# Haar coefficients left unscaled, thresholds scaled on the chip, products copied by ScalarE

## The chip, the core and the metric

The kernel runs on one core of a Trainium2 chip. The metric is the device time of one execution in microseconds (us). A core has a matrix engine (TensorE, PE in the profile), three engines for elementwise work (VectorE or DVE, ScalarE or ACT, GpSimd or POOL), and SyncE (SP), which here issues all transfers. Sixteen DMA engines carry them. TensorE writes to PSUM, and another engine has to copy the result from there to SBUF, the on-chip memory.

## The reference

The input is x with 4 images, 64 channels and 256 x 256 points in float32. Four layers follow each other. Layers 0, 2 and 3 are long convolutions with a filter that is a product of a row part and a column part; the filters come from a small network with sines:

```python
k = jnp.einsum('ijk,imk->ijmk', hx, hy)[0]           # per channel: a column times a row
y = irfft2(rfft2(x) * rfft2(k) / fft_size)[..., :L, :L]
out = y + x * bias[:, None, None]
```

Layer 1 works on Haar wavelet coefficients. The 2D transform is orthonormal (a factor of 1/sqrt(2) at each of its 8 steps along rows and along columns); channels are mixed with two weight matrices, and the result is shrunk by soft thresholds that differ from point to point but not from channel to channel:

```python
f1 = haar2d(x)
for i in range(2):
    f4 = jnp.einsum('bchw,oc->bohw', f1 * v[i], conv_w[i])
    acc = acc + jnp.sign(f4) * jax.nn.relu(jnp.abs(f4) - tau[i])
y = haar2d(acc, inverse=True) + x
```

## The kernel before

The images form two groups of two. Phase A does layer 0 and the forward Haar transform; phase B does the mixing and the shrinking; phase C does the inverse transform and layers 2 and 3. Between the phases the coefficients go through DRAM (`coef` from A to B, `mixed` and `unshrunk` from B to C), because A and C work by channel and B by position.

**Phase A** has 64 rounds, 32 for each group; a round has 2 channels of 2 images. A round multiplies by Toeplitz matrices on TensorE, first along one axis (PSUM tiles `a1ps`, copied by ScalarE to `ay`, L460), then along the other (`a2ps`, joined with the bias term by VectorE into `x`, L480). Then GpSimd does the Haar transform along the free axis (`forward_free`, L360 and L362), with sums and differences only, and a product with a 64 x 64 Haar matrix (`a3ps`, L324) does most of the other axis. Each of its four PSUM tiles a round is evicted into `f` by `product` (L493), and four DMAs (two in group 1) store `f` to `coef` (L497). The free-axis factors that GpSimd leaves out depend only on the column; `wrow_sb` holds them, one for each of 256 columns, and L493 multiplies by it.

The pieces of a round are written out by hand as lists of small functions, and `beside` interleaves one list with another by count. `later` puts an eviction into the next piece. A piece that issues a DMA does so on SyncE, in program order: an issue that has to wait for a buffer or for data keeps back all later ones. In a round SyncE issues four loads of x (L148, 2 KB rows in group 0), four loads of Toeplitz rows `toep` (L161, 32 partitions each) and the stores of `coef`. While phase A works on group 0, the list `rest` runs beside it: the networks of layers 2 and 3 and twelve stores (`spread`, L278) that write each filter to DRAM in repeated copies.

**Phase B** has 64 steps for each group, two units a step (the two weight matrices). For each step it loads `ft` (512 KB, L564) and a tile `v` with the weights v and the thresholds tau (L577). The host has repeated both for the 64 channels; a row of `in_v` holds v and tau of both units in turn. A unit is: product with the mixing weights (L623), times v (VectorE, L642), sign and magnitude (ScalarE, L648 and L657), minus tau and maximum times sign (VectorE, L662 and L667), sum (GpSimd, L682 to L686), store to `mixed` (L691). For group 1 the second unit of most steps is stored raw (L639, L699) and shrunk later, in phase C, with `v_rows`.

**Phase C** reads `mixed` (L774), scales column levels on ScalarE (`scales`, L378), does the inverse transform on GpSimd (`inverse_free`, L401; on VectorE for the first two rounds, L403) and the two convolutions on TensorE.

Phase A of group 0 runs first, then A of group 1 beside B of group 0, then C of group 0 beside B of group 1, and last C of group 1.

Of the kernel before, what the change touches and what calls it, by code (L numbers as in the profile page):

```python
# [97 lines left out]

@with_exitstack
def conv_haar_kernel(  # L100
    ctx: ExitStack, tc: tile.TileContext, x, zT, w1, wbd, cols, wo, decay, wo_first, decay_first, bias, forward, inverse, wrow, pack, v, v_rows, out
):
    nc = tc.nc
    ctx.enter_context(tc.manual_schedule())
# [180 lines left out]
    nc.sync.dma_start(forward_sb, forward)  # L285
    inverse_sb = const.tile([P, ROW], F32, tag="inverse", name="inverse_sb")
    nc.sync.dma_start(inverse_sb, inverse)
    wrow_sb = const.tile([P, N], F32, tag="wrow", name="wrow_sb")
    nc.sync.dma_start(wrow_sb, wrow.partition_broadcast(P))
    bias_sb = const.tile([P, NL * C], F32, tag="bias", name="bias_sb")  # L290
    nc.sync.dma_start(bias_sb, bias.partition_broadcast(P))

    for p in network([0]):
        p()

    rest = []
    rest.append(lambda: wbd_sb.extend(constant(f"wbd{l}", wbd[:, l], [P, 2, P]) for l in (1, 2)))
# [7 lines left out]
    def half(r):  # L305
        return slice(r * ROW, (r + 1) * ROW)

    def toeplitz(ps, data, t, j):

# [61 lines left out]
        m = half // BLOCKS  # L371
        return src.rearrange("p n (k q) -> p (n k) q", k=BLOCKS)[:, :, m : 2 * m]

    def scales(src):

        half = 2
        while half < N:
            nc.scalar.mul(diffs(src, half), diffs(src, half), math.sqrt(half))  # L378
            yield
            half *= 2  # L380

    def inverse_free(src, dst, name, engine, level):
# [27 lines left out]
    def later(op):  # L410

        waiting.append(op)
# [23 lines left out]
    def phase_a():  # L436


        total = GROUPS * ROUNDS
        st = [dict() for _ in range(total)]  # L440

        def filters(t):
            if t < total:
                st[t]["toep"] = first_toep[t] if t < len(first_toep) else load_toeplitz(0, t)

        def load(t):
            if t < total:
                st[t]["x"] = first_x[t] if t < len(first_x) else load_x(t)

        def rows(t, j):  # L450
            s = st[t]
            if j == 0:
                s["y"] = big("t0", f"ay_{t}", 2)
            if j % 2 == 0:
                s["ps"] = banks(f"a1ps{j}_{t}")
            toeplitz(s["ps"], blocks(s["x"]), filters_x(s["toep"]), j)
            if j % 2:
                for r, ps in enumerate(s["ps"]):
                    y = blocks(s["y"])[:, r, j - 1 : j + 1]
                    later(lambda y=y, ps=ps: nc.scalar.copy(y, ps))  # L460

        def columns(t, j):
            s = st[t]
            if j == 0:
                s["x1"] = big("m0", f"x1_{t}", 2)
            if j % 2 == 0:
                s["ps2"] = banks(f"a2ps{j}_{t}")
            toeplitz(s["ps2"], blocks(s["y"]), filters_y(s["toep"]), j)
            if j % 2:
                for e, ps in enumerate(s["ps2"]):  # L470
                    later(lambda e=e, ps=ps: residual(t, e, j, ps))
            if j == BLOCKS - 1:
                s["fw"] = big("m1", f"fw_{t}", 2)
                s["ops"] = forward_free(s["x1"], s["fw"], f"f{t}_")

        def residual(t, e, j, ps):
            s = st[t]
            c = t % ROUNDS * CI + e
            to, old = (blocks(s[name])[:, e, j - 1 : j + 1] for name in ("x1", "x"))
            nc.vector.scalar_tensor_tensor(to, old, bias_sb[:, c : c + 1], ps, ALU.mult, ALU.add)  # L480

        def product(t, bp):
            s = st[t]
            if bp == 0:

                s["f"] = big("out", f"f_{t}", 2)
            two = banks(f"a3ps{bp}_{t}")
            fw = blocks(s["fw"])
            haar(two, lambda r, c: fw[half(r), c, 2 * bp : 2 * bp + 2], forward_sb)
            for b, ps in enumerate(two):  # L490
                f = s["f"][:, 4 * bp + 2 * b : 4 * bp + 2 * b + 2]
                w = wrow_sb.unsqueeze(1).to_broadcast([P, 2, N])
                later(lambda f=f, ps=ps, w=w: nc.vector.tensor_tensor(f, ps, w, ALU.mult))  # L493

        def store(t):
            for to, f in all_rows(coef[t // ROUNDS], t % ROUNDS, st[t]["f"], t >= ROUNDS):
                nc.sync.dma_start(to, f)  # L497
# [36 lines left out]
        t = total - 1  # L534
        end = [lambda: (flush(), run(st[t]["ops"], 16), store(t - 1))]
        end += [lambda bp=bp: (flush(), product(t, bp)) for bp in range(2)]
        end.append(lambda: (flush(), store(t)))
        return pieces, last, end

    def phase_b(grp):  # L540
# [25 lines left out]
        def load_v(s):  # L566
            if s >= STEPS:
                return
            d = st[s]
            d["v"], d["tau"] = [], []  # L570

            def fetch(first, count, tag):
                n = 2 * count * W
# [4 lines left out]
                d["v"] += [t[:, i, 0] for i in range(count)]  # L578
                d["tau"] += [t[:, i, 1] for i in range(count)]
# [176 lines left out]
    def phase_c():  # L756
# [29 lines left out]

        def scale_rows():
            for k in range(2):
                for op in scales(late["rows"][:, k].rearrange("p s (h k) -> p (s h) k", h=2)):
                    pass  # L790

        def shrink(t, k):
# [353 lines left out]
```

## Time and profile before

| | |
|---|---|
| median of 3 runs | 2545.4 us (2540.11 to 2548.39) |
| profiled execution | 2543.18 us, span 2541.3 us |
| mean granted TensorE clock | 0.979 |
| PE, PEld busy | 2311.6 us (91%), 1875.9 us (74%) |
| DVE, ACT, POOL busy | 1840.0 (72%), 1325.9 (52%), 2063.0 us (81%) |
| transfers | 679.08 MB, 267 GB/s on average |
| L493, the multiplication by `wrow_sb` | 256 on VectorE, 161.3 us, 682 ns each |
| `v<-in_v` | 64 of 1024 KB (group 0), 64 of 512 KB (group 1) |

The busy share of an engine is an average over four stages with different limits, so the stages have to be read one by one: a window of the trace gives each engine's busy time in that stretch, the clock that TensorE was granted, the mean busy share of the 16 DMA engines, and what they moved. Idle time of an engine that doesn't set the pace costs nothing. SyncE's issue times show when a transfer was asked for, not when it moved.

### The profile page before, as it was taken

The numbers are of one execution on the slowest core, as the hardware profiler recorded it, in microseconds if no ns is written. First come the engines' busy times: TensorE is split into PE (matmuls) and PEld (weight loads), VectorE is DVE, ScalarE is ACT, GpSimd is POOL, SyncE is SP. The second block draws the span as 40 slices with busy tenths as digits, with TensorE's granted clock in tenths as the row PEclk, the third lists the DMA queues.
The fourth block names the chain that finished last, engine by engine and source line by source line (L and its number), as shares of the span: only waits on it lengthen the run. The fifth ranks groups of instructions, "written<-read, shape, count | busy, mean of one in ns | idle before, by whom it ended". The sixth has DMA issues, their size and how long they took to land.

```text
span 2541.3 us, 118857 instructions
## 1 busy us (share of the span) xinstructions
PE 2311.6 (91%) x53298; PEld 1875.9 (74%) x53298; DVE 1840.0 (72%) x2070; ACT 1325.9 (52%) x2190; POOL 2063.0 (81%) x2428
## 2 busy tenths in 40 slices
PE   7999998788888888877999999999989999999999
PEld 5799996444454444555777777787889999998888
DVE  4655557799999999856777677776667777777763
ACT  1122223566666666244666666666655555556552
POOL 2889997989899999768777767676779999999990
PEclk9999999899999999888999999999999999999999
DMA  6678877799999999556888889889866666666653
GB/s 201 224 269 271 272 275 296 266 327 338 337 320 341 336 318 340 206 184 248 318 320 313 306 302 321 311 312 315 287 215 217 216 215 217 215 212 207 220 167 111
DMA packets 201798, 679.08 MB, mean 267 GB/s; under 512 B 29119, under 2 KB 30464, under 8 KB 188873
## 3 DMA queue, kind: packets, MB, share of 16 engines
q1 hardware_dynamic: 201288, 671.48, 76.3%
q8 instruction: 419, 6.86, 1.1%
q14 instruction: 91, 0.74, 0.1%
HBM read 427.63 MB, written 243.73 MB: 264 GB/s over the span
## 4 chain that ended last, share of the span: by engine, by line
PE 44%; DVE 4%; issue 2%; ACT 2%; DMA 2%; POOL 2%; SPq 1%; DVEq 0%; ACTq 0%; POOLq 0%
PE c2c L312 10%; PE c2r L312 10%; PE c1r L312 9%; PE c1c L312 8%; PE c0ps L324 4%; PE f L623 3%; DVE cy L896 1%; DVE m L667 1%; DMA g<-mixed 1%; DVE x L642 1%; DVE x L662 1%; ACT ch L877 1%; POOL i L401 1%; ACT x L657 0%; SPq L161 0%
## 5 line engine op out<-in xcount | busy, mean ns | idle before, releaser
L401 POOL TENSOR_TENSOR i<-i,g 128x16 f32<-128x16 f32 x744 | 429.9, 598 | 28.2 <-ACT g L378 1.1
L312 PEld LDWEIGHTS a2ps<-toep,ay 64*64 64x64 f32 x8192 | 315.3, 136 | 126.3 <-DVE f L493 70.0
L623 PE MATMUL f<-ft,mix 64*64 64x512 f32 x2048 | 301.7, 623 | 116.8 <-DVE x L642 99.2
L312 PE MATMUL a2ps<-toep,ay 64*64 64x128 f32 (+3 forms) x8192 | 352.8, 303 | 27.4 <-DVE f L493 27.4
L312 PEld LDWEIGHTS a1ps<-toep,x 64*64 64x64 f32 x8192 | 300.1, 134 | 66.3 <-issue 31.8
L312 PE MATMUL a1ps<-toep,x 64*64 64x64 f32 (+3 forms) x8192 | 338.1, 299 | 4.3 <-DMA toep<-filt 2.3
L312 PEld LDWEIGHTS c2c<-toep,ch 64*64 64x64 f32 x8192 | 296.8, 135 | 61.0 <-issue 28.4
L312 PEld LDWEIGHTS c1c<-toep,ch 64*64 64x64 f32 x8192 | 295.4, 133 | 52.0 <-issue 23.7
L685 POOL TENSOR_TENSOR gt<-m,ft 128x512 f32<-128x512 f32 x128 | 163.3, 1276 | 197.8 <-DVE m L667 193.5
L312 PE MATMUL c1r<-toep,z 64*64 64x64 f32 (+3 forms) x8192 | 315.0, 300 | 7.8 <-issue 3.8
L312 PEld LDWEIGHTS c1r<-toep,z 64*64 64x64 f32 x8192 | 291.2, 135 | 41.5 <-issue 19.0
L312 PE MATMUL c2c<-toep,ch 64*64 64x128 f32 (+3 forms) x8192 | 310.0, 299 | 8.6 <-ACT ch L877 6.9
L312 PE MATMUL c2r<-toep,cy 64*64 64x128 f32 (+3 forms) x8192 | 310.1, 298 | 7.9 <-issue 6.6
L312 PEld LDWEIGHTS c2r<-toep,cy 64*64 64x64 f32 x8192 | 288.9, 134 | 37.6 <-issue 20.4
L401 POOL TENSOR_TENSOR ci<-i,g 128x1024 f32<-128x1024 f32 x124 | 312.1, 2539 | 4.5
L648 ACT ACTIVATE m<-x 128x1024 f32<-128x1024 f32 x194 | 206.0, 1062 | 210.0 <-DVE x L642 103.1
L312 PE MATMUL c1c<-toep,ch 64*64 64x128 f32 (+3 forms) x8192 | 307.3, 297 | 4.1 <-ACT ch L877 2.5
L460 ACT COPY ay<-a1ps 128x512 f32<-128x512 f32 x256 | 137.3, 589 | 325.2 <-PE a1ps L312 324.6
L877 ACT COPY ch<-c2r 128x512 f32<-128x512 f32 x256 | 137.2, 589 | 285.2 <-PE c2r L312 284.4
L493 DVE TENSOR_TENSOR f<-a3ps,wrow_sb 128x512 f32<-128x512 f32 x256 | 161.3, 682 | 122.5 <-PE a3ps L324 118.6
L642 DVE TENSOR_TENSOR x<-f,v 128x1024 f32<-128x1024 f32 x192 | 233.4, 1216 | 18.1 <-PE f L623 15.3
L896 DVE SCALAR_TENSOR_TENSOR o<-cy,bias_sb,c2c 128x512 f32<-128x512 f32 x256 | 176.9, 742 | 91.8 <-PE c2c L312 87.1
(84 smaller groups left out, 3950.7 us busy)
## 6 DMA issues: line engine op xcount, KB each, us to landing
toep<-filt SPq DMA_DIRECT2D x768, 112.0 KB
ft<-coef SPq DMA_DIRECT2D x128, 512.0 KB
v<-in_v SPq DMA_DIRECT2D x64, 1024.0 KB
mixed<-gt SPq DMA_DIRECT2D x128, 512.0 KB
g<-mixed SPq DMA_DIRECT2D x256, 256.0 KB
x<-in_x SPq DMA_DIRECT2D x128, 256.0 KB
coef<-f SPq DMA_DIRECT2D x128, 256.0 KB
x<-in_x SPq DMA_DIRECT2D x32, 1024.0 KB
```

Of the source, the lines that this page charges most:

```text
L312: nc.tensor.matmul(ps[r][half(c), j % 2, k * ROW :], data[half(r), c, k, bass.ts(j, ROW)], t(r, c)[:, : N - k * ROW], start=k == 0, stop=k ...
L324: nc.tensor.matmul(ps[r][half(c)].rearrange("p h k -> p (h k)"), matrix[half(r)], pairs(r, c).rearrange("p h k -> p (h k)"), start=True, s ...
L401: engine.tensor_tensor(to, s, d, op)
L460: later(lambda y=y, ps=ps: nc.scalar.copy(y, ps))
L493: later(lambda f=f, ps=ps, w=w: nc.vector.tensor_tensor(f, ps, w, ALU.mult))
L623: nc.tensor.matmul(un[u]["f4"][half(q), b, :], mixers[0][half(r), bass.ts(i, C)], st[s]["f"][half(r), b], start=True, stop=True, tile_posi ...
L642: nc.vector.tensor_tensor(un[u]["x"], un[u]["f4"], both(u, "v"), ALU.mult)
L648: nc.scalar.activation(un[u]["m"], un[u]["x"], AF.Sign)
L662: nc.vector.tensor_tensor(un[u]["a"], un[u]["a"], both(u, "tau"), ALU.subtract)
L685: nc.gpsimd.tensor_tensor(g[:, 0], m[:, 0], st[s]["f"][:, 0], ALU.add)
L877: later(lambda y=y, ps=ps: nc.scalar.copy(y, ps))
L896: nc.vector.scalar_tensor_tensor(to, of, bias_sb[:, at : at + 1], ps, ALU.mult, ALU.add)
```

## The change

Coefficients now go to `coef` without the scale of their column level. The host divides the rows of the Haar matrix by sqrt(256) in its place, and `scales` and `inverse_free` use half instead of sqrt(half). So the product needs no multiplication any more, and ScalarE copies it. The shrinking has to use thresholds divided by the missing scale: the host passes tau once, for 128 rows, and the factors `per_level`; VectorE multiplies them once, early in phase A, and 64 stores put the result into a new DRAM tensor `thresholds` for each of the 64 channels, interleaved with the list `rest` by the new function `merged`. Phase B loads v and the thresholds with two DMAs instead of one. `wrow` is gone; `in_v` holds v alone.

```diff
+    thresholds = dram.tile([STEPS, 2, C, 2 * W + PAD], F32, tag="thresholds", name="thresholds")
...
-    wrow_sb = const.tile([P, N], F32, tag="wrow", name="wrow_sb")
-    nc.sync.dma_start(wrow_sb, wrow.partition_broadcast(P))
...
+    def merged(one, other):
+        both = [((k + 0.5) / len(of), p) for of in (one, other) for k, p in enumerate(of)]
+        return [p for _, p in sorted(both, key=lambda x: x[0])]
...
+    tau_sb = mp.tile([P, 2, W], F32, tag="tau", name="tau_sb")
+    def scale_thresholds():
+        per_level_sb = mp.tile([P, N], F32, tag="per_level", name="per_level_sb")
+        nc.sync.dma_start(per_level_sb, per_level.partition_broadcast(P))
+        nc.sync.dma_start(tau_sb.rearrange("p r w -> p (r w)"), tau)
+        rows = tau_sb.rearrange("p r (h k) -> p (r h) k", k=N)
+        nc.vector.tensor_tensor(rows, rows, per_level_sb.unsqueeze(1).to_broadcast([P, 4, N]), ALU.mult)
+    def put_thresholds(copies, r, i):
+        of = tau_sb[half(i), r].unsqueeze(1).to_broadcast([ROW, copies.stop - copies.start, W])
+        nc.sync.dma_start(thresholds[:, r, copies, i * W : (i + 1) * W], of)
+    puts = [(slice(n, n + 4), r, i) for n in range(0, C, 4) for r in range(2) for i in range(2)]
+    rest = merged(rest, [scale_thresholds] + [lambda at=at: put_thresholds(*at) for at in puts])
...
-    def scales(src):
+    def scales(src, power=1.0):
...
-            nc.scalar.mul(diffs(src, half), diffs(src, half), math.sqrt(half))
+            nc.scalar.mul(diffs(src, half), diffs(src, half), half**power)
...
-                    engine.scalar_tensor_tensor(to, d, math.sqrt(half) * (1 - 2 * q), s, ALU.mult, ALU.add)
+                    engine.scalar_tensor_tensor(to, d, float(half * (1 - 2 * q)), s, ALU.mult, ALU.add)
...
-                w = wrow_sb.unsqueeze(1).to_broadcast([P, 2, N])
-                later(lambda f=f, ps=ps, w=w: nc.vector.tensor_tensor(f, ps, w, ALU.mult))
+                later(lambda f=f, ps=ps: nc.scalar.copy(f, ps))
...
-                t = bp.tile([P, count, 2, W], F32, tag=tag, name=f"{tag}_{grp}_{first}_{s}", bufs=3)
-                at = v.offset + s * P * (4 * W + PAD) + first * 2 * W
-                rows = bass.AP(v.tensor, at, [[4 * W + PAD, P], [1, n]])
-                nc.sync.dma_start(t.rearrange("p i k w -> p (i k w)"), rows)
+                t = bp.tile([P, 2, count, W], F32, tag=tag, name=f"{tag}_{grp}_{first}_{s}", bufs=3)
+                at = slice(first * W, (first + count) * W)
+                nc.sync.dma_start(t[:, 0].rearrange("p i w -> p (i w)"), v[s, :, at])
+                nc.sync.dma_start(t[:, 1].rearrange("p i w -> p (i w)"), thresholds[s].rearrange("r c w -> (r c) w")[:, at])
...
-    signs = signs * w[order][:ROW, None]
+    signs = signs * w[order][:ROW, None] / math.sqrt(N)
```

More of the change, by code (lines that the diff above doesn't have):

```diff
@@ L100, in conv_haar_kernel @@
 def conv_haar_kernel(
-    ctx: ExitStack, tc: tile.TileContext, x, zT, w1, wbd, cols, wo, decay, wo_first, decay_first, bias, forward, inverse, wrow, pack, v, v_rows, out
+    ctx: ExitStack, tc: tile.TileContext, x, zT, w1, wbd, cols, wo, decay, wo_first, decay_first, bias, forward, inverse, pack, v, tau, per_level, v_rows, out
 ):
@@ L294, in conv_haar_kernel, with half @@
         p()
+    def half(r):
+        return slice(r * ROW, (r + 1) * ROW)
+    def merged(one, other):
+        both = [((k + 0.5) / len(of), p) for of in (one, other) for k, p in enumerate(of)]
+        return [p for _, p in sorted(both, key=lambda x: x[0])]
     rest = []
@@ L572, in fetch @@
             def fetch(first, count, tag):
-                n = 2 * count * W
-                t = bp.tile([P, count, 2, W], F32, tag=tag, name=f"{tag}_{grp}_{first}_{s}", bufs=3)
-                at = v.offset + s * P * (4 * W + PAD) + first * 2 * W
-                rows = bass.AP(v.tensor, at, [[4 * W + PAD, P], [1, n]])
-                nc.sync.dma_start(t.rearrange("p i k w -> p (i k w)"), rows)
-                d["v"] += [t[:, i, 0] for i in range(count)]
-                d["tau"] += [t[:, i, 1] for i in range(count)]
+                t = bp.tile([P, 2, count, W], F32, tag=tag, name=f"{tag}_{grp}_{first}_{s}", bufs=3)
+                at = slice(first * W, (first + count) * W)
+                nc.sync.dma_start(t[:, 0].rearrange("p i w -> p (i w)"), v[s, :, at])
+                nc.sync.dma_start(t[:, 1].rearrange("p i w -> p (i w)"), thresholds[s].rearrange("r c w -> (r c) w")[:, at])
+                d["v"] += [t[:, 0, i] for i in range(count)]
+                d["tau"] += [t[:, 1, i] for i in range(count)]
             fetch(0, 2 if grp < GROUPS - 1 else 1, "v")
@@ L788, in scale_rows @@
             for k in range(2):
-                for op in scales(late["rows"][:, k].rearrange("p s (h k) -> p (s h) k", h=2)):
+                for op in scales(late["rows"][:, k].rearrange("p s (h k) -> p (s h) k", h=2), (1.0, 0.5)[k]):
                     pass
@@ L1090 @@
     scaled = signs * w[order][:ROW, None] / math.sqrt(N)
-    signs = signs * w[order][:ROW, None]
+    signs = signs * w[order][:ROW, None] / math.sqrt(N)
     pack = a["L1_conv_conv_w"].transpose(2, 0, 1).reshape(C, P)
-    v = np.stack([by_row("v"), by_row("tau")], axis=3)
     filters = [[[r * CI, r * CI + 1, C + r * CI + h] for h in range(2)] for r in range(ROUNDS)]
@@ L1129 @@
         "inverse": f(np.concatenate([scaled] * 2).astype(np.float32)),
-        "wrow": f(w[order].astype(np.float32)),
         "pack": f(np.concatenate([pack, pack])),
-        "v": padded(np.repeat(v[:, :, None], C, axis=2).reshape(STEPS * P, 4 * W)),
+        "v": padded(np.repeat(by_row("v")[:, :, None], C, axis=2).reshape(STEPS, P, 2 * W)),
+        "tau": f(by_row("tau").transpose(2, 0, 1, 3).reshape(P, 2 * W)),
+        "per_level": f((1.0 / (w[order] * math.sqrt(N))).astype(np.float32)),
         "v_rows": f(np.stack([by_block("v"), by_block("tau")], axis=1)),
```

2 lines of the change are left out of this document (removed).

## The prediction

> **What bounds the kernel now.** I read the page's 40 slices first, to see that stages have different limits. Then the windows of each stage, then the transfer queue, and last the group, the waits and the issue times that the change touches. The slices, each 63.5 us (busy tenths; GB/s for all transfer engines):
>
> ```profile
> DVE  4655557799999999856777677776667777777763
> POOL 2889997989899999768777767676779999999990
> DMA  6678877799999999556888889889866666666653
> ```
>
> VectorE, GpSimd and the transfers are all near full only in slices 8 to 15. The windows are by stage: start:end, length, then PE, PEld, DVE, ACT and POOL busy us with instruction counts, TensorE clock, DMA share, GB/s.
>
> ```profile
> 120.00:360.00 240.00, 240.00 (x6226) 225.89 (x6222) 120.99 (x184) 49.40 (x92) 214.60 (x365) 1.00 0.79 269
> 480.00:1020.00 540.00, 441.38 (x7160) 263.00 (x7152) 516.17 (x528) 350.67 (x436) 489.84 (x539) 0.98 0.95 333
> 1200.00:1800.00 600.00, 560.34 (x13197) 467.06 (x13201) 435.20 (x411) 383.88 (x667) 428.67 (x485) 1.00 0.89 313
> 1800.00:2541.00 741.00, 728.12 (x19843) 660.92 (x19834) 505.61 (x572) 406.48 (x770) 622.80 (x627) 1.00 0.63 206
> ```
>
> Call these stages A1 (phase A alone, about 25 to 409 us), A2 (phase A beside B of group 0, about 420 to 1030), C1 (phase C beside B of group 1) and C2. A1 is TensorE's: busy 240 of 240 us, VectorE half idle. In A2 VectorE is busy 96%, but the transfers 95% too. The changed multiplication (L493) beside a ScalarE copy of the same shape (L460), from the page's groups; then A2's waits (total us, times, longest):
>
> ```profile
> L460 ACT COPY ay<-a1ps 128x512 f32<-128x512 f32 x256 | 137.3, 589 | 325.2 <-PE a1ps L312 324.6
> L493 DVE TENSOR_TENSOR f<-a3ps,wrow_sb 128x512 f32<-128x512 f32 x256 | 161.3, 682 | 122.5 <-PE a3ps L324 118.6
> ```
>
> ```profile
> ACT m L648 <- POOL gt L682: 59.1, 35, 2.2
> PEld a2ps L312 <- DVE f L493: 56.1, 77, 2.0
> PE a2ps L312 <- DVE f L493: 19.7, 23, 1.1
> ```
>
> TensorE waits 76 us in A2 for L493, yet has 99 us of slack there; what VectorE is short of is its own time.
>
> **ScalarE copies the products (A1 and A2).** 256 x 682 ns leave VectorE, 256 x 589 ns come to ScalarE. In A1 that gives nothing: TensorE is full, and ScalarE goes from 49 to 103 us of 240 (23 rounds x 4 x 0.589). In A2, 540 us are 23 rounds, hence 92 multiplications, 62.7 us of VectorE; over the stage's 610 us 71 us. That is the gain if VectorE alone sets A2. GpSimd is at 489.84 of 540, so 9% is the most before it is full, and the transfers leave only 5%: 30 us of 610. They have no visible stall on the compute engines now, so they keep pace but with little over. I take 3%, -18 us, because transfers are nearest to full; ends 0 and -45 (GpSimd full at 98%: 540 to 500 us, scaled to 610). What is late next is a load, v or x. ScalarE grows from 351 to 405 us of 540 and stays covered. Behind each copy in its queue stand sign and magnitude, on which VectorE waits, but the copy's wait on TensorE ends while ScalarE is idle a third of the time.
>
> **Thresholds written per channel (A1).** New are 64 stores `thresholds<-tau_sb`, 64 partitions x 4 copies x 2 KB = 512 KB each, 33.6 MB, spread evenly over 32 rounds: two a round, one beside each round's x loads and one beside its coefficient stores. All go through SyncE's one queue, where the loads of the next rounds stand behind them. No store like this is timed in the trace. The nearest is `filt<-padded` (L278), also SBUF to DRAM, from 64 neighbouring partitions, each row repeated. SyncE's issues around one (start, us), and the windows in which each moves:
>
> ```profile
> 201.43 2.83 SPq L161 DMA_DIRECT2D toep<-filt  x4
> 204.31 0.63 SPq L278 DMA_DIRECT2D filt<-padded  x1
> 205.04 4.01 SPq L497 DMA_DIRECT2D coef<-f  x4
> 209.34 2.57 SPq L148 DMA_DIRECT2D x<-in_x  x4
> 212.01 2.83 SPq L161 DMA_DIRECT2D toep<-filt  x4
> ```
>
> ```profile
> 206.00:208.00 2.00, 2.00 (x67) 2.00 (x63) 1.28 (x3) 0.00 (x0) 1.76 (x7) 1.00 1.00 240
> 212.00:214.00 2.00, 2.00 (x32) 1.74 (x28) 1.05 (x2) 1.07 (x2) 1.92 (x2) 1.00 1.03 380
> 214.00:216.00 2.00, 2.00 (x68) 2.00 (x64) 1.43 (x3) 0.00 (x0) 1.92 (x4) 1.00 0.57 168
> ```
>
> The L278 store fills all engines (1.00) and moves only 240 GB/s (249 at the next one, 226 to 228 us); x, over 128 partitions, moves 380; the toep loads of 32 partitions keep about half the engines busy (0.57, 168 GB/s). So a put costs 524 KB / 240 = 2.18 us at one end, 524 / 380 = 1.38 at the other. I take 2.0, nearer to the row of the same form.
>
> [...]
>
> What room is there? 92 toep loads in A1's 240 us are 23 rounds of 10.43 us. The share of 0.79 leaves 21%, 2.16 us a round. But one round's four toep loads (459 KB at 168 GB/s) take 2.73 us with 43% of the engines idle, 1.17 us of those 2.16, and that idle time lies on one half of the engines. On the busier half 0.99 us is left. Room is thus 0.99 to 2.16; I take 1.6, as a queue that is always full hides some start-up gaps. Two puts cost 4.0 us, 2.4 more than the room; of 32 rounds the first three lie in the fill, so 29 x 2.4 = **+70 us**. Ends: 29 x (2 x 1.38 - 2.16) = +17, and 29 x (2 x 2.18 - 0.99) = +97. The bound of A1 moves from TensorE to the transfers, and TensorE waits for x and toep.
>
> **Scaling them once.** Two loads (640 KB) and one VectorE multiplication of 128x1024 (the nearest, L642, 1.22 us) at about 40 us. The first put waits for it, and behind that put on SyncE stand the next toep and x loads, needed about 15 us later. A stall of 0 to 8 us (the load's way through a queue that already moves x and filters, then 1.22); I take +3. VectorE waits for the load as well, while it has only 0.76 to 2.62 us of work in each 4 us between 36 and 52 us: inside the same 3. Phase B's loads of `thresholds` wait for the puts, but the last put is issued three rounds (31 us) before A1 ends: 0, and up to the +8 above if the queue is that far behind.
>
> **v and tau by two loads (A2, C1).** In A2 one 1024 KB load of 8 KB rows becomes two of 4 KB rows; in C1 one of 4 KB rows becomes two of 2 KB rows; 64 + 64 + 2 more issues, 0.53 us each, on a SyncE that waits much of A2 for buffers anyway. Rate per full share: A2 now 333/0.95 = 350 GB/s with 8 KB rows, C1 313/0.89 = 352 with 4 KB rows, so A2 pays nothing that I can see (ends -5, +5). A1, a third of its bytes in 2 KB rows (88 x loads of 256 KB in its 240 us), has 269/0.79 = 341: 3% worse. 64 x 512 KB = 33.6 MB in C1 cost 96 us at 350 and 98.7 at 341: **+3** (ends -3, +8), as TensorE has little slack there.
>
> **The rest.** The constants in `scales`, `inverse_free` and the Haar matrix change values, not instructions; the 128 KB of wrow go, less than 1 us early on. C2 keeps its instructions: 0.
>
> **Sum.** +70 + 3 - 18 + 3 = +58 on the profiled execution, 2543.2 us (span 2541.3), gives 2601. The median before is 2545.4, 2 more: forecast **2603 us**. Under 0.3% (7.6 us) a measurement of this kernel can't tell from no change.
>
> **Rivals.** (1) *The puts run at L278's rate and A2 gains nothing.* A1 +97, start +8, A2 +5, C1 +8: +118, 2663. For it: the same form of store, and A2's transfers at 0.95. Against: a full queue is denser than the A1 of now. (2) *The copies get stuck on ScalarE.* The sign ahead of a copy waits up to 2.2 us for GpSimd to free m, and TensorE then waits for a bank. Two pairs a round x 2.2 = 4.4 us, against TensorE's slack of 99 / 23 = 4.3 a round; it decides only if nearly every pair is hit. Then the 76 us of waits for f grow instead of shrinking; if they double and a quarter of the increase lands on the path, A2 has +20: 70 + 3 + 20 + 3 = +96, 2641. (3) *Faster: the puts fit into the idle share, and A2 is VectorE's alone.* One mechanism, transfers with room: a put at 1.38 us and the idle 2.16 us usable on all engines make A1 +17, and A2 goes down to GpSimd's limit, -45; C1 -3. -31, 2514. It decides where a round's put time falls below about 3.5 us with the room at 2.16 and A2 can use the 5% and denser packets. Against it: the 240 GB/s, and the toep loads on half the engines. (4) *Even:* +17 in A1, -18 in A2: no change. That the change doesn't do what it says is no case of weight: ScalarE's list holds the 256 copies and SyncE's the 64 puts.
>
> **How the numbers follow.** Forecast 0.48, rival 1 0.22, rival 2 0.11, rival 3 0.13, rival 4 0.06. Slower 0.48 + 0.22 + 0.11 = 0.81, same 0.06, faster 0.13. The range runs from 2540, just below no change, to 2665, just above rival 1; it leaves out rival 3 (0.13) and the upper part of rival 1.
>
> **What would show it.** In the profile after: DMA share in A1 near 1.0; A1 rounds of some 12.8 us instead of 10.43, with TensorE waiting for `x<-in_x` or `toep<-filt`; the first `ft<-coef` issue, at 398 us before, some 70 later. While puts move, windows of share 1.0 at about 250 GB/s. In A2 VectorE near 85%, transfers at 0.97 or more, and 22.8 instead of 23.5 us a round. C2 as long as before. I am wrong if A1's TensorE stays full (puts are free), if A2 shortens by over 45 us (VectorE was alone), or if A2 lengthens with TensorE waiting for ScalarE's f.

## The result, and the profile after

The changed kernel takes 2670.7 us (median of 4 runs, 2662.6 to 2672.25) against 2543.1 us of the kernel before (4 runs): a ratio of 1.0493, 95% interval 1.0463 to 1.0522. It is 128 us slower. The profiled execution took 2662.6 us with a span of 2660.8, which is 119.5 above the span before. Forecast were 2603 us and a range from 2540 to 2665.

The span is cut by three events that both traces have: the first mixing product `f<-ft` (end of A1), the first copy `ch<-c1r` (end of A2), and the last mixing product (end of C1). In us, read from the tiles' first and last times:

| | A1 | A2 | C1 | C2 | span |
|---|---|---|---|---|---|
| before | 409.3 | 680.3 | 736.1 | 715.6 | 2541.3 |
| after | 518.9 | 703.4 | 722.9 | 715.6 | 2660.8 |
| difference | +109.6 | +23.1 | -13.2 | 0 | +119.5 |

This is the part of the page after with the 40 slices, now 66.5 us each, busy share in tenths:

```profile
DVE  4421221367787888865677777777757777777763
POOL 1776766688888888986867887776869999999991
DMA  6888998869889999975699999988976666666653
```

In slices 2 to 7 VectorE falls to between 1 and 3 and the transfers stand at 8 or 9, where before they were at 7 and 8. In slices 8 to 16, which are mostly A2, VectorE has 6 to 8, where before it had 9. The windows after show A1, A2, C1 and C2 (start:end, length, then PE, PEld, DVE, ACT and POOL busy with instruction counts, granted TensorE clock, DMA share, GB/s):

```profile
120.00:420.00 300.00, 256.21 (x5829) 232.66 (x5825) 61.52 (x90) 88.58 (x173) 207.37 (x350) 0.95 0.90 277
540.00:1080.00 540.00, 411.85 (x6687) 283.66 (x6684) 430.84 (x404) 363.80 (x487) 464.30 (x504) 0.90 0.88 306
1320.00:1920.00 600.00, 569.89 (x13460) 462.93 (x13456) 441.30 (x416) 388.06 (x676) 453.31 (x493) 0.99 0.90 321
1920.00:2660.00 740.00, 727.97 (x19831) 691.88 (x19821) 505.57 (x572) 406.61 (x770) 621.79 (x627) 0.99 0.62 205
```

In A1 TensorE is busy 256 of 300 us instead of all the time. The transfers are at 0.90 for 277 GB/s: a larger share for hardly more bytes a second than the 0.79 and 269 GB/s before. In A2 nothing is near full: VectorE 80% (it was 96%), GpSimd 86% (it was 91%), transfers 0.88 (they were 0.95). ScalarE has 67%, up from 65. A stage that got longer while no engine is full is held by waits between engines, so the waits are what to read.

In A1, the transfer view of 120 to 420 us (queue: packets, MB, share of 16 engines; then the issues and KB each):

```profile
q1 hardware_dynamic: 35821, 82.38, 88.5%
thresholds<-tau_sb SPq DMA_DIRECT2D x44, 512.0 KB
toep<-filt SPq DMA_DIRECT2D x84, 112.0 KB
```

A round has four toep loads, so 84 are 21 rounds of 14.3 us, where before a round took 10.43. The waits of the same stretch (total us, times, longest) and SyncE's issues of most of a round:

```profile
PE a1ps L335 <- DMA x<-in_x: 34.6, 27, 4.2
PEld a1ps L335 <- DMA x<-in_x: 27.0, 21, 3.5
```

```profile
300.53 0.63 SPq L324 DMA_DIRECT2D thresholds<-tau_sb  x1
301.26 4.35 SPq L519 DMA_DIRECT2D coef<-f  x4
305.71 2.87 SPq L149 DMA_DIRECT2D x<-in_x  x4
308.63 0.65 SPq L324 DMA_DIRECT2D thresholds<-tau_sb  x1
309.37 3.95 SPq L162 DMA_DIRECT2D toep<-filt  x4
```

Each put stands ahead of transfers that a round needs, and TensorE waits for x. In A2 the waits from 600 to 1140 us are these:

```profile
PEld a2ps L335 <- ACT f L515: 92.0, 44, 5.8
PE a2ps L335 <- ACT f L515: 68.3, 22, 4.9
DVE x L663 <- PE f L644: 30.5, 13, 3.4
ACT m L669 <- POOL gt L703: 25.0, 26, 2.1
```

The matmuls (PE) wait 68 us for `f` where they waited 20 before, the weight loads (PEld) 92 where they waited 56; the longest single waits are 4.9 and 5.8 us instead of 1.1 and 2.0. The two rows run beside each other, as the next view shows, so they must not be added. One of the waits in order of time (start, us; in brackets the idle time before, and what ended it):

```profile
798.81 1.56 PE L347 MATMUL a3ps<-fw,forward_sb 64*64 64x512 f32 x8
...
801.37 1.06 ACT L669 ACTIVATE m<-x 128x1024 f32<-128x1024 f32 x1 [2.13 <-POOL gt L703]
...
802.33 1.01 ACT L678 ACTIVATE a<-x 128x1024 f32<-128x1024 f32 x1
...
803.37 1.24 ACT L694 COPY other<-ft 64x512 f32<-64x512 f32 x2
...
804.63 2.05 ACT L515 COPY f<-a3ps 128x512 f32<-128x512 f32 x4
...
805.27 0.29 PEld L335 LDWEIGHTS a2ps<-toep,ay 64*64 64x64 f32 x4 [5.79 <-ACT f L515]
805.27 2.46 PE L335 MATMUL a2ps<-toep,ay 64*64 64x256 f32 x26 [4.91 <-ACT f L515]
```

The product `a3ps` is there at 800.4. Its copy is queued one piece later, behind the sign (which waits 2.1 us until GpSimd has read the last `m`), the magnitude and two exchange copies into `other` (they swap the two halves of the partitions), and so starts at 804.6, 4.3 us late. TensorE needs the bank (the part of PSUM that holds the product) for the next one, and its matmuls stand for 4.9 us.

### The profile page after: what moved, and what is told of

Same layout as the page of the kernel before. It is cut to its first block, busy times and chain, and to the rows that moved or that the text cites. A ratio compares the mean times of both kernels' runs of the same rounds, so it can differ in the third digit from the quotient of the medians.

```text
span 2660.8 us, 119293 instructions
## 1 busy us (share of the span) xinstructions
PE 2345.7 (88%) x53298; PEld 1968.7 (74%) x53298; DVE 1697.0 (64%) x1815; ACT 1449.9 (54%) x2446; POOL 2076.9 (78%) x2428
## 4 chain that ended last, share of the span: by engine, by line
PE 42%; DVE 4%; DMA 2%; issue 2%; POOL 2%; ACT 2%; SPq 1%; DVEq 0%; ACTq 0%; POOLq 0%
PE c2c L335 9%; PE c2r L335 9%; PE c1r L335 8%; PE c1c L335 8%; PE c0ps L347 3%; PE f L644 3%; DVE cy L917 1%; DVE m L688 1%; DVE x L683 1%; DVE x L663 1%; DMA g<-mixed 1%; POOL i L424 1%; DMA toep<-filt 0%; DMA unshrunk<-raw 0%; SPq L162 0%
## 5 line engine op out<-in xcount | busy, mean ns | idle before, releaser
L335 PEld LDWEIGHTS a2ps<-toep,ay 64*64 64x64 f32 x8192 | 362.7, 144 | 152.9 <-ACT f L515 114.8
L335 PE MATMUL a2ps<-toep,ay 64*64 64x64 f32 (+3 forms) x8192 | 373.5, 319 | 86.1 <-ACT f L515 82.3
L335 PE MATMUL a1ps<-toep,x 64*64 64x256 f32 (+3 forms) x8192 | 369.7, 313 | 65.1 <-DMA x<-in_x 46.9
L335 PEld LDWEIGHTS a1ps<-toep,x 64*64 64x64 f32 x8192 | 329.0, 141 | 130.8 <-issue 73.9
L644 PE MATMUL f<-ft,mix 64*64 64x512 f32 x2048 | 316.3, 635 | 92.4 <-DVE x L663 72.2
L503 DVE SCALAR_TENSOR_TENSOR x<-x,bias_sb,a2ps 128x512 f32<-128x512 f32 x256 | 179.4, 742 | 330.7 <-POOL f L385 128.4
L335 PE MATMUL c1r<-toep,z 64*64 64x256 f32 (+3 forms) x8192 | 313.4, 299 | 3.9 <-ACT z L886 1.8
L335 PE MATMUL c1c<-toep,ch 64*64 64x256 f32 (+3 forms) x8192 | 309.6, 297 | 5.1 <-ACT ch L898 2.7
L335 PE MATMUL c2r<-toep,cy 64*64 64x256 f32 (+3 forms) x8192 | 309.8, 297 | 2.4 <-issue 1.8
L383 POOL TENSOR_TENSOR fw<-x 128x1024 f32<-128x1024 f32 x64 | 121.7, 1902 | 220.2 <-DVE x L503 216.2
```

The source lines that it names most:

```text
L335: nc.tensor.matmul(ps[r][half(c), j % 2, k * ROW :], data[half(r), c, k, bass.ts(j, ROW)], t(r, c)[:, : N - k * ROW], start=k == 0, stop=k ...
L383: nc.gpsimd.tensor_tensor(diffs, even, odd, ALU.subtract)
L644: nc.tensor.matmul(un[u]["f4"][half(q), b, :], mixers[0][half(r), bass.ts(i, C)], st[s]["f"][half(r), b], start=True, stop=True, tile_posi ...
```

## The experiments

Stage lengths in us, by the same three events, and the times. The number of runs is in brackets; a ratio needs several. The stage lengths are those of one trace each: in the nine traces without puts and scaling, before among them, A1 lies between 409 and 416 us, so a few us there mean little.

| run | A1 | A2 | C1 | C2 | time (runs) | ratio to before |
|---|---|---|---|---|---|---|
| e1_no_puts | 412.2 | 703.9 | 727.6 | 717.1 | 2564.4 (6) | 1.0066 (1.0042 to 1.0089) |
| e2_puts_128 | 456.6 | 704.2 | 731.0 | 715.6 | 2609.2 (1) | |
| e3_dve_copy | 514.8 | 681.1 | 729.3 | 716.5 | 2643.6 (1) | |
| e4_before_split | 411.0 | 680.8 | 724.9 | 716.6 | 2541.2 (10) | 0.9974 (0.9957 to 0.999) |
| e5_copy_now | 411.1 | 667.2 | 724.0 | 717.0 | 2521.1 (1) | |
| e6_half_half | 411.8 | 698.3 | 723.3 | 716.3 | 2551.5 (1) | |
| e7_no_tau_load | 411.4 | 704.6 | 725.9 | 714.9 | 2558.7 (1) | |
| e8_puts_act | 496.8 | 704.1 | 725.6 | 716.7 | 2645.0 (1) | |
| e9_small_thresholds | 421.8 | 730.6 | 739.0 | 720.6 | 2604.8 (6) | 1.0237 (1.0209 to 1.0265) |
| e10_before_now | 413.2 | 667.1 | 728.1 | 717.0 | 2527.1 (1) | |
| e11_add_on_dve | 413.6 | 695.2 | 719.1 | 718.4 | 2548.1 (1) | |
| e12_split_now | 416.3 | 666.1 | 720.2 | 720.6 | 2524.2 (6) | 0.9903 (0.988 to 0.9927) |
| e13_both_mended | 455.2 | 667.3 | 721.5 | 719.0 | 2565.9 (5) | 1.0089 (1.0061 to 1.0118) |
| e14_mended_act | 451.0 | 666.1 | 723.5 | 719.1 | 2561.9 (1) | |

### Phase A: the puts

**No puts.** The changed kernel without the scaling and the 64 stores; phase B reads thresholds that the host has repeated, not divided by the scale.

```diff
-    rest = merged(rest, [scale_thresholds] + [lambda at=at: put_thresholds(*at) for at in puts])
+        "thresholds": padded(np.repeat(by_row("tau")[:, :, None], C, axis=2).reshape(STEPS, 2, C, 2 * W)),
```

> This kernel leaves out the division of the thresholds: they come from the host undivided and already repeated per channel, so the 64 puts, the two loads and the one multiplication before them are gone; all else is as in the changed kernel. Stage lengths (start to first mixing product; from there to the first ScalarE copy of phase C; from there to the last mixing product; rest) are 409.3 / 680.3 / 736.1 / 715.6 us before and 518.9 / 703.4 / 722.9 / 715.6 after. Theory P (the puts alone lengthen the first stage; the ScalarE copies lengthen the second): 409 to 414, 703, 723, 716, in all about 2553. Rival S (ScalarE's copies also slow the first stage, and the puts are only part of it): first stage over 430. Rival T (the second stage is longer because the puts' backlog or the thresholds' place in DRAM disturbs it): second stage back to 680, in all about 2530.

Window of this kernel:

```profile
120.00:420.00 300.00, 294.81 (x7485) 266.34 (x7481) 85.41 (x130) 112.60 (x219) 258.07 (x442) 0.99 0.80 272
```

A1 is 412.2 us and TensorE is nearly full again (295 of 300 us): 107 of the 110 us are the scaling and the puts. A2 keeps its 704 us, so its loss comes from another part.

**The same bytes from every other partition.** Each put reads 64 rows of `tau_sb` that lie in partitions 0, 2, 4 and so on, instead of 64 neighbouring ones; the host lays tau out to fit.

```diff
-        of = tau_sb[half(i), r].unsqueeze(1).to_broadcast([ROW, copies.stop - copies.start, W])
+        every = tau_sb.rearrange("(s i) r w -> i s r w", i=2)[i]
+        of = every[:, r].unsqueeze(1).to_broadcast([ROW, copies.stop - copies.start, W])
```

> Same 64 puts of 512 KB with the same rows, copies and DRAM addresses, but the 64 source rows of a put lie in every other partition of all 128 instead of in 64 neighbouring ones. Theory P (a put is slow, about 2.17 us of all engines, because its 64 neighbouring partitions are served at 240 GB/s): a put falls to about 1.4 us, two puts a round save 1.5 of the 14.3 us, and the first stage goes from 518.9 to about 470 (nearly 30 rounds), in all about 2615. Rival R (it is the bytes, the 2 KB rows or the writing in DRAM that cost): first stage stays within 510 to 520.

```profile
120.00:420.00 300.00, 278.30 (x6763) 250.04 (x6752) 70.43 (x102) 102.79 (x200) 235.41 (x400) 0.98 0.91 320
```

With nearly the same share (0.91, it was 0.90) the engines now move 320 GB/s instead of 277, and A1 falls by 62 us to 456.6. So 58% of the 107 us lie in where the source rows lie, and 44 remain. The bytes and the destination are the same, only the source partitions differ; why 64 neighbouring ones are slower isn't shown.

**Issued from ScalarE's queue.** One word: the store is issued by ScalarE, so that x, toep and `coef` no longer stand behind it on SyncE.

```diff
-        nc.sync.dma_start(thresholds[:, r, copies, i * W : (i + 1) * W], of)
+        nc.scalar.dma_start(thresholds[:, r, copies, i * W : (i + 1) * W], of)
```

> The changed kernel with its 64 puts issued from ScalarE's queue instead of SyncE's; rows, bytes and source partitions as in the changed kernel. In the first stage SyncE is never idle after the change: its issues fill the 14.3 us of a round. Theory P (the transfer engines are what is full, and SyncE's issues only stretch because they are held back): first stage 510 to 525. Rival Y (SyncE's queue is full of issues, or a load stands behind a put in it): first stage 470 or less.

```profile
120.00:420.00 300.00, 262.47 (x6078) 225.17 (x6070) 66.36 (x96) 91.13 (x177) 210.56 (x362) 0.95 0.92 287
```

A1 is 496.8, between what the two theories named: with slow puts, 22 us were the order in one queue, and most of the loss stays. The 22 us are a balance. TensorE's matmuls now wait 7 us for x instead of 35 (120 to 420 us), but 10 us for ScalarE's `ay`, a wait that the trace after doesn't have.

### Phase A beside B: the copies

**The copy on VectorE.** The changed kernel with the copy in the place of the old multiplication.

```diff
-                later(lambda f=f, ps=ps: nc.scalar.copy(f, ps))
+                later(lambda f=f, ps=ps: nc.vector.tensor_copy(f, ps))
```

> The changed kernel with its 256 copies of the Haar products on VectorE instead of ScalarE. Theory P (the copies stand in ScalarE's queue behind signs and magnitudes, and TensorE waits for them): second stage back to about 680 or, as the first stage's end and the transfers stay the same, between 675 and 685; first stage 519 as before this edit; in all about 2640. Rival D (the second stage is longer because v and the thresholds come in two transfers): it stays at 700 or goes above it, in all 2660 or more.

A2 is 681.1, as before the change; A1 keeps its loss. So the +23 us are the copies on ScalarE.

**The copy right behind its product.** As e1, but ScalarE's copy is queued at once, not one piece later.

```diff
-                later(lambda f=f, ps=ps: nc.scalar.copy(f, ps))
+                nc.scalar.copy(f, ps)
```

> Leaves out the division of the thresholds, as the run without puts did, so the first stage is free of the puts; the ScalarE copies of the Haar products are queued right after their product instead of one piece later, ahead of the signs, magnitudes and exchanges of the one or two units that come between. Second stage without puts: 703.9 us with ScalarE copies, 680.8 in the kernel before. Theory Q (TensorE waits for PSUM banks because the copies stand behind those operations in ScalarE's queue): its waits for f (165 us in 540) fall by half or more, and the second stage goes to 685 or below, with VectorE's 63 us gained perhaps to 665. Rival H (ScalarE then stands blocked at the copy until TensorE has finished the product, and the signs and magnitudes behind it are late): 704 or more. Rival X (transfers or clock set the stage): 700 to 708, waits for f gone but others in their place.

Window, then waits from 520 to 1060 us:

```profile
520.00:1060.00 540.00, 429.24 (x7360) 271.65 (x7356) 458.80 (x442) 382.58 (x519) 490.25 (x549) 0.97 0.93 326
```

```profile
PEld a2ps L317 <- ACT f L497: 23.0, 63, 1.2
PE a2ps L317 <- ACT f L497: 5.4, 5, 1.1
PE f L626 <- DVE x L645: 87.7, 83, 2.8
```

The same work on the same engine: the matmuls' wait for `f` falls from 59 us (e1, 560 to 1100 us) to 5, the longest from 4.9 to 1.1, and A2 from 703.9 to 667.2, which is 13 us less than before the change. The place in ScalarE's queue was the fault, not the engine. TensorE's largest wait is now the one for VectorE's product with v (the last line).

**Half of the copies on each engine.** As e1, one copy of each pair on VectorE, still one piece late.

```diff
-                later(lambda f=f, ps=ps: nc.scalar.copy(f, ps))
+                copy = nc.vector.tensor_copy if b else nc.scalar.copy
+                later(lambda f=f, ps=ps, copy=copy: copy(f, ps))
```

> Leaves out the division of the thresholds, as the run without puts did; of each pair of Haar products one is copied by ScalarE and one by VectorE. Theory Q: a product's banks come free only with the later of the two, so TensorE still waits for ScalarE; but ScalarE's row of copies is half as long: second stage between 681 and 704, about 692. Rival V (VectorE's time alone sets the stage and ScalarE's queue does no harm): below 680. Rival X (transfers): 704 as with all copies on ScalarE.

```profile
520.00:1060.00 540.00, 430.89 (x7011) 270.93 (x7007) 471.43 (x465) 356.06 (x461) 474.32 (x520) 0.89 0.91 315
```

A2 is 698.3: halving ScalarE's share brought 6 of the 23 us. That fits a wait which one late copy of a pair is enough to cause; no run tests that alone.

**Without the thresholds' loads.** As e1, and phase B uses v where tau was, so that a third of phase B's load bytes is gone in A2.

```diff
-                nc.sync.dma_start(t[:, 1].rearrange("p i w -> p (i w)"), thresholds[s].rearrange("r c w -> (r c) w")[:, at])
-                d["tau"] += [t[:, 1, i] for i in range(count)]
+                d["tau"] += [t[:, 0, i] for i in range(count)]
```

> The run without puts, with the loads of the thresholds left out as well: v stands in for them, so 33.6 MB less move in the second stage and 33.6 MB less in the third. ScalarE copies as in the changed kernel. Theory Q (ScalarE's queue order sets the second stage): it stays at 698 to 706 although the transfers fall from a share of 0.89 to about 0.75. Rival X (the transfers, at 0.89 to 0.95 and more on half of the engines, set it once VectorE is relieved): 680 or below, perhaps 640. Third stage: if its transfers set it (0.89 to 0.92), 690 or below; if TensorE does, 720 to 730.

```profile
520.00:1060.00 540.00, 417.62 (x6832) 285.73 (x6826) 443.03 (x415) 374.34 (x501) 466.88 (x509) 0.91 0.76 261
```

The transfers' share falls to 0.76, and A2 is 704.6 against 703.9. With the copies late, transfers don't set A2. In C1 the loads lose 64 x 256 KB, 16.8 MB (not the 33.6 that was expected); the share there falls from 0.91 to 0.84 (1230 to 1830 us in e1, to 1800 here), and C1 is 725.9 against 727.6. So transfers don't set C1 either.

**The old multiplication right behind its product.** The kernel before, with one edit.

```diff
-                later(lambda f=f, ps=ps, w=w: nc.vector.tensor_tensor(f, ps, w, ALU.mult))
+                nc.vector.tensor_tensor(f, ps, w, ALU.mult)
```

> The kernel before with its multiplication on VectorE queued right after the product instead of one piece later; nothing else. If the earlier place alone made the second stage shorter (theory O), it falls from 680.3 to about 667 here too, in all about 2530. If it is the 63 us taken off VectorE that shorten it, and the place only lets them count (theory Q), VectorE at 96 per cent keeps it at 677 to 685, or longer where VectorE stands blocked at the multiplication, in all 2538 to 2560.

```profile
520.00:1060.00 540.00, 432.87 (x7422) 274.93 (x7416) 512.39 (x540) 336.28 (x423) 492.81 (x551) 0.97 0.94 329
```

A2 is 667.1, the same as with the copies on ScalarE (667.2), although VectorE is busy 95% here and 85% there. Once it is queued at once, taking the multiplication from VectorE is worth nothing that can be seen; queueing it one piece earlier is worth 13 us.

**One of GpSimd's sums on VectorE.** As e5; the sum of the second image in group 0 (L686 in the kernel before) moves from GpSimd.

```diff
-                nc.gpsimd.tensor_tensor(g[:, 1], m[:, 1], st[s]["other"], ALU.add)
+                engine = nc.vector if grp == 0 else nc.gpsimd
+                engine.tensor_tensor(g[:, 1], m[:, 1], st[s]["other"], ALU.add)
```

> The run without puts and with the copies queued right after their product (667.2 us in the second stage; it leaves out the division of the thresholds), with one more edit: for group 0 the sum of the second image (64 instructions of 128x512, 1.28 us each on GpSimd) goes to VectorE, which has the room that the ScalarE copies made. Theory G (GpSimd sets the second stage: busy 490 to 499 of 540 us there in all versions, and its waits, some 27 us for x and 6 to 13 others, fill nearly all the rest, so time taken from VectorE alone is worth nothing): GpSimd loses 82 us, VectorE gets some 42, second stage 600 to 640. Rival V (VectorE or its order with ScalarE sets it): 667 or more. Rival X (transfers, 0.93 there): 645 to 660, share 0.97 or more.

The window, and the moved sum in the groups of that stretch (count | busy us, mean ns | idle before):

```profile
520.00:1060.00 540.00, 415.19 (x6874) 261.21 (x6868) 501.80 (x473) 375.12 (x503) 412.57 (x463) 0.94 0.90 314
```

```profile
L690 DVE TENSOR_TENSOR gt<-m,other 128x512 f32<-128x512 f32 x55 | 66.7, 1213 | 0.0
```

GpSimd's load falls from 490 to 413 us, yet A2 grows to 695.2, so theory G's 600 to 640 didn't come. But the edit loads VectorE at the same time: the sum takes 1213 ns there on average (680 to 2472), VectorE goes from 459 to 502 us, and the matmuls' wait for its product with v from 88 to 107 us. So the run doesn't tell whether GpSimd's time holds A2 at 667; what does stays open.

### The loads, and repairs

**v and tau in two loads, alone.** The kernel before with separate inputs.

```diff
-                nc.sync.dma_start(t.rearrange("p i k w -> p (i k w)"), rows)
+                nc.sync.dma_start(t[:, 0].rearrange("p i w -> p (i w)"), v[s, :, at])
+                nc.sync.dma_start(t[:, 1].rearrange("p i w -> p (i w)"), thresholds[s].rearrange("r c w -> (r c) w")[:, at])
```

> The kernel before, with v and tau as two inputs and two transfers for each load instead of one (nothing else). Theory P: first stage 409, second 680 to 685, fourth 716; the third shows whether the two transfers are what shortened it by 13 us: 723 then, in all about 2530, faster than before. Rival N (the third stage varies by ten us with how the two phases happen to meet, whatever is loaded how): 730 to 740, in all 2541 to 2547. Rival D (two transfers lengthen the second stage): second stage near 703, in all about 2565.

The ratio is 0.9974, 0.1 to 0.4% faster; in its trace C1 is 724.9 instead of 736.1. C1 alone scatters: 728.1 with one load in e10, 719 to 731 with two in most others. The gain is small, and it rests on the whole time.

**Thresholds stored once.** A complete kernel: 512 KB are stored instead of 33.6 MB, phase B's loads read each row for all 64 channels (two loads of 64 neighbouring partitions instead of one of 128), and the copies follow their products at once.

```diff
+        nc.sync.dma_start(thresholds[:, :, i * W : (i + 1) * W], tau_sb[half(i)])
+                for r in range(2):
+                    row = bass.AP(thresholds.tensor, thresholds.offset + (2 * s + r) * 2 * W + first * W, [[0, C], [1, count * W]])
+                    nc.sync.dma_start(t[half(r), 1].rearrange("p i w -> p (i w)"), row)
```

> A whole kernel that computes all of the reference: the divided thresholds are written to DRAM once (two stores, 512 KB in all) and not per channel; phase B's load reads one row for the 64 partitions of its half (two loads of 64 partitions in place of one of 128); ScalarE's copies are queued right after their product. Theory Q with P (no puts to speak of in the first stage; copies not stuck in the second; transfers not the limit of the second and third): stages 412 / 668 / 725 / 716, in all about 2523, 0.8 per cent faster than before. Rival K (64 partitions that read one and the same row, and 64 to 128 more issues on SyncE, hold up the loads): second stage 680 or more, or third over 736, in all 2540 or more.

Window, and one wait of that stretch:

```profile
520.00:1060.00 540.00, 395.63 (x6428) 240.81 (x6428) 417.33 (x391) 354.10 (x474) 441.76 (x488) 0.89 0.98 300
```

```profile
DVE x L663 <- DMA v<-in_v: 82.9, 37, 6.1
```

A1 is nearly cured (421.8), but A2 grows by 63 us over e5: the transfers are full (0.98) at only 300 GB/s, and VectorE waits 83 us for v. The cost moved from the stores to the loads, as rival K said. (The trace is of the longest of the six runs, 9 us above their median.) Whether it is the row read 64 times isn't shown: each load now also goes to 64 neighbouring partitions, the form that was slow in the puts. At that form's 240 GB/s instead of 350 the 104 loads of 256 KB in the window would take some 36 us more, an estimate from the L278 row and the rates before. A load of one row into all 128 partitions, or into every other one, wasn't run.

**Two loads and the multiplication at once.** A complete kernel: e4 with the edit of e10.

```diff
-                later(lambda f=f, ps=ps, w=w: nc.vector.tensor_tensor(f, ps, w, ALU.mult))
+                nc.vector.tensor_tensor(f, ps, w, ALU.mult)
```

> A whole kernel: the kernel before, with v and tau in two transfers and the multiplication on VectorE queued right after its product. Sum of the two single results: stages 412 / 667 / 727 / 716, in all 2523, 0.8 per cent faster than before. If the two overlap (the two transfers and the earlier place each shift the same thing), 2527 to 2535.

The ratio is 0.9903 (0.988 to 0.9927): 24 us faster than the kernel before on the same chip (2548.2). It beats both kernels, and it has nothing of the change but the two loads.

**Both faults of the change mended.** The changed kernel with the edits of e2 and e5, complete.

```diff
-        of = tau_sb[half(i), r].unsqueeze(1).to_broadcast([ROW, copies.stop - copies.start, W])
+        every = tau_sb.rearrange("(s i) r w -> i s r w", i=2)[i]
+        of = every[:, r].unsqueeze(1).to_broadcast([ROW, copies.stop - copies.start, W])
...
-                later(lambda f=f, ps=ps: nc.scalar.copy(f, ps))
+                nc.scalar.copy(f, ps)
```

> The complete changed kernel with both repairs: the puts read 64 rows in every other partition, and ScalarE's copy is queued right behind its product instead of one piece later. If the two faults of the change are separate, the stage lengths are taken over from the runs that mended one of them: A1 457 (alternate partitions), A2 667 (copy at once), C1 about 725, C2 716: span about 2565, against 2541 of the kernel before, a ratio of 1.009. Rival, the faults interact (a late end of phase A leaves its stores in SyncE's queue and delays the loads of A2, or the store order changes with the earlier copies): A2 above 680, or A1 off 457 by more than 6; then the sum of the single repairs is not the repair of the whole.

The stages are 455.2, 667.3, 721.5 and 719.0 us, against 457, 667, 725 and 716 expected. The two faults are separate, and their repairs add up. With both, the change still costs 0.9%.

**And the puts from ScalarE's queue.** As e13, with the edit of e8.

```diff
-        nc.sync.dma_start(thresholds[:, r, copies, i * W : (i + 1) * W], of)
+        nc.scalar.dma_start(thresholds[:, r, copies, i * W : (i + 1) * W], of)
```

> As the kernel with both repairs, and the 64 puts issued from ScalarE's queue instead of SyncE's. Theory: what is left of the puts' price with alternate partitions, about 45 us in A1, is the time of their bytes on the 16 engines, and the order of the issues adds little once a put is short: A1 445 to 457. Rival: the order behind SyncE's puts is a cost of its own, as large as the 22 us that it was worth with the slow puts: A1 about 435, span about 2543, level with the kernel before.

A1 is 451.0: 4 us less, not 22, and 4 is within what A1 differs by from trace to trace. Moving the puts off SyncE paid only while a put was slow. Some 39 us over e1 remain:

```profile
120.00:420.00 300.00, 282.79 (x6952) 242.72 (x6946) 74.11 (x108) 104.09 (x202) 238.73 (x406) 0.99 0.93 327
```

The transfers are at 0.93 here, and TensorE is busy 283 of 300 us. What is left is, I take it, mostly the time of 33.6 MB on engines that e1 already keeps at 0.80; no run takes it apart further.

## Why the prediction was right and wrong

Two steps failed. The one whose mechanism was wrong is A2: ScalarE "stays covered", -18 us, where the copies' place in its queue cost +23. The other is the size of the puts in A1: +73 with the scaling, where it was +107.

**The bound of A1** moved to the transfers as forecast, and TensorE waits for x. The term was +70, with the scaling +73, and e1 shows +107 for both together. The share stood at 0.90, though, not near 1.0 as I had written, and a round took 14.3 us, not 12.8. Two factors of the term were off. The first is the put's price. The idle share left after is 100 - 88.5 - 1.0 - 0.1 = 10.4% (the last two are the instruction queues), 1.49 us of a 14.3 us round, so only 2.16 - 1.49 = 0.67 us of the idle time was used. The round grew by 3.86 us, so 2.1 puts a round (44 in 21) cost 4.53 us, or 2.16 us each: the upper end, the rate of the L278 row (2.18). I took 2.0 because x moves faster (380 GB/s, against 240 in the row); the row of the same form was the answer. The same sum for e2 (25 rounds of 12.0 us, 49 puts, 8.7% idle) gives 1.37 us a put, the price at the rate of x, which spans 128 partitions (1.38).

The second factor, and the larger, is the room. I took 1.6 us of a round, above the lower end of 0.99, on the assumption that a full queue hides gaps, which no run shows. The 0.99 itself was an estimate from the share of 0.57 in one window of toep loads: that it is always the same engines that stand idle there was inferred, not read. The puts used 0.67, less than that lower end; in e2 they used 1.12. That x, toep, `coef` and puts are issued in turn on one queue is part of it: with the puts on another queue A1 lost 22 us (e8). How the engines come to stand idle in between isn't shown.

**Scaling once** was +3, and that was too little. SyncE stands 4.8 us at the first put until `tau_sb` is scaled, and VectorE waits 22.6 us for the load of `tau_sb`. The first three rounds take 40.1 us after and 27.3 in e1, read from the starts of ScalarE's copies `ay`; the first puts fall into the same time. e9 has the scaling with no put near it: VectorE waits 9.9 us there, and A1 is 421.8 against 411.1 in e5, of which some us may be scatter. In any case the rounds of the fill, for which I counted no put, weren't free.

**A2** was -18 and became +23. Rival 2 named the place, ScalarE's queue, and I gave it 0.11 because it seemed to need nearly every pair to be hit. It counted 2.2 us for a pair, the sign's wait for GpSimd, and set two such waits against the slack averaged over a round (4.3). But that wait isn't what grew: it falls from 59 us before to 25 after. At 800 us only 1.0 of the copy's 4.3 us of lateness is the rest of the sign's wait; the sign, the magnitude and the two exchange copies themselves are the other 3.3, and TensorE needs the bank inside the round. An average of slack says nothing of a bank that is needed at one moment. The rival's price, +20, was close, but by luck: it was a quarter of a doubled 76 us, and the 76 add the waits of matmuls and weight loads, which run side by side. Its statement of what would show it, TensorE waiting for ScalarE's f, is what the waits show. The other half of the step was wrong too: VectorE, 96% busy, looked like A2's bound, and e10 against e5 shows that its 63 us are worth nothing there once the eviction is queued at once. With late copies it isn't the transfers either, which I took as the next limit (e7); in e5 they stand at 0.93, and no run tests them there.

The granted clock in A2 is 0.90 after and 0.97 in e5. Whether it falls because TensorE stands, or adds to the length, isn't parted by these runs. The copy's place alone doesn't decide it: e9, with the copy at once and the matmuls waiting for VectorE instead, has 0.89.

**C1** was +3, and the trace shows -13, of which e4's interval (2 to 11 us of the whole time) supports a part. The reason for the +3 didn't hold: e7 shows that transfers don't set C1. **C2** was 0 and is 0. The sum was +58 and the spans give +119.5, a miss of 62: 37 in A1 (110 for 73, the scaling included), 41 in A2, less 16 in C1, which nothing in the prediction foresaw. The rest of the 68 us between forecast and median is that the median after lies 8 us above its profiled execution, where I allowed 2.

## What to carry over

Ask of every operation that changes its engine what stands ahead of it in the new engine's queue, and who waits for its buffer at that moment; compare a single wait with the slack at that point, not with the mean slack of a round. An engine that is busy 96% isn't yet the bound: queueing its work earlier brought 13 us, taking that work away as well brought nothing more. For a transfer that the trace doesn't have, take the rate of the row with the same side and the same partitions (2.16 us a put here, 2.18 by the row), and count little of the idle transfer time as usable: here it was 0.67 of 2.16 us a round, less than my lower end.

## What the runs showed of the hardware

- Stores whose 64 source rows lie in neighbouring partitions cost 2.16 us per 512 KB, worked out from round length and transfer share; from every other partition, by the same sum, 1.37 us (e2). With 64 stores A1 is 62 us shorter.
- With loads that read one row in DRAM for 64 neighbouring partitions, A2's transfers are full (share 0.98) at 300 GB/s (e9); with repeated rows and 128 partitions they moved 326 GB/s at 0.93 (e5). Which of the two differences costs isn't parted.
- A 128x512 sum out of SBUF on VectorE took between 680 and 2472 ns, 1213 on average (e11), while the multiplication of the same shape out of PSUM took 620 to 693 ns before. What lengthens the sums isn't shown.
